# Small squares' additions and a low-part subtraction on VectorE, and a new layout of the period, in a three-layer float32 kernel

## The chip, the cores and the metric

The kernel runs on one core of a Trainium2 chip. A core has a matrix engine (TensorE, PE in the profile; its weight loads are shown apart as PEld), a vector engine (VectorE, DVE), an engine for functions of one operand (ScalarE, ACT), a general one (GpSimd, POOL) and a queue for transfers (SyncE, SP). Each works through its own list of instructions in order, and semaphores tie the lists together. The metric is the device time of one execution in microseconds.

## The reference, cut to what matters

The input x has 8 elements of 512 tokens by 256 channels, all float32. Four residual layers follow one another:

```python
x = x + attn_a(layernorm(x))   # 16 heads of 64, attention among the 64 channels of one token's head
x = x + ffn(layernorm(x))      # silu gate 256->1024, two gelu layers 1024->1024, 1024->256
x = x + attn_b(layernorm(x))   # ordinary causal attention over 512 tokens, 16 heads of 16
x = x + ffn(layernorm(x))
```

The first attention is the unusual one. For every token and head it forms a 64 by 64 matrix of products q[i]*k[j], keeps the lower triangle (j <= i), takes its softmax along j and multiplies by v:

```python
scores = einsum('bshq,bshk->bshqk', Q, K);  scores[upper triangle] = -inf
attn   = einsum('bshqk,bshk->bshq', softmax(scores), V)
```

This is no matrix product: each token has a triangle of its own, so nearly all of it is elementwise work on VectorE, GpSimd and ScalarE. The other layers are mostly matrix products.

## The kernel before

**Tiles and periods.** In the first attention, 128 tokens lie on the 128 partitions. A *period* is the work on one tile of 128 tokens (i, 4 per element) and one group of 4 heads (g, 4 per element). So an element b has 16 periods, and the kernel 128. Element 0 uses one layout (`'first'`), elements 1 to 7 another (`'order'`).

**Squares.** The triangle is cut into its diagonal and squares below it: in each head one square of 32 by 32, two of 16, four of 8, and so on to 32 of 1. `units` (line 597) packs them in four units: unit 0 is the squares of 32 of heads 0 and 1, unit 1 the squares of 16 of all four heads, unit 2 the squares of 32 of heads 2 and 3, and unit 3 all squares of 8, 4, 2 and 1. For each unit the steps are `scores` (products q*k; on GpSimd for units 0, 1 and 2, on VectorE for unit 3), `exps` (ScalarE), `weigh` (times v, on VectorE), then the sums along j. The tile `acc` gathers for each query the denominator (half 0) and the numerator (half 1).

**Sums.** Units 0 to 2 are first halved by `halve`, an adding DMA that GpSimd issues (line 861). After that:
- Unit 0 has the kind `'pe16'` (`'sum': ['pe16', 'dve']`): `sums32` adds by 16 transposing matmuls into PSUM (line 882), ScalarE copies (944), PE transposes back (953), and VectorE's `add32` adds the PSUM result into `acc` (964).
- Unit 2 has the kind `'dve'` in elements 1 to 7: `fold` on GpSimd (869), `gather` on VectorE (1002), addition on GpSimd through `adds` and `add_rows` (1016). In element 0 it is `'pe16'` as well.
- Unit 1: `gather` on VectorE, and `adds` on GpSimd.
- Unit 3: squares of 8 and 4 go through `gather` on VectorE and `adds` on GpSimd. For those of 2 and 1, `small_squares` needs no reduction: GpSimd adds the two halves of the squares of 2 (line 987) and adds both results into `acc` (line 1016, rows named `acc<-acc,ws`).

Then `invert` (a reciprocal on VectorE, 1022), `divide` (GpSimd, 1028), two transposes on PE (`turn_group`, 1038), and the output projection (`project_out`, `new_x`). All transposes and projections of this layer share one PSUM tile, `bank`, of two halves.

**The order.** The program is written out by a table. An entry `[slot, what, ...]` says that this step of period n is issued in slot 12*n + slot. All periods overlap, and within one slot the steps go in the order of the table:

```python
n, r = divmod(t - slot, 12)
if r == 0 and lo <= n < hi:
    now.append((place / len(order), what, self.todo[n] + args))
```

Between the slots a generator hands out the other three layers of the previous element (`after_a`, line 1534), paced so that they keep step with the periods; in one element the PE passes through gate products (1229), hidden products (1301), the second attention (1380 to 1503), then a second gate and hidden stretch. An engine's queue is therefore the interleaving of both, fixed when the program is built.

**The gate.** For each of 8 blocks of a feed-forward layer, ScalarE takes silu (1205), VectorE multiplies (1208), ScalarE rounds a high part (1212), and the low part, what was lost in rounding, is a subtraction of 128x512 (1213), on GpSimd. `later` puts each of these steps one flush after the one before. The same pattern in the hidden layers has its subtraction on VectorE (1267).

Of the kernel before, what the change touches and what calls it, by code (L numbers as in the profile page):

```python
# [13 lines left out]
ALU = mybir.AluOpType  # L14
# [5 lines left out]
NB, S, D = 8, 512, 256  # L20
# [22 lines left out]
G = {'sum': ['pe16', 'dve'],  # L43
 'p16': 2,
 'rot': 4,
 'half': [0, 0, 0, 0, 1, 1],
 'order': [[12, 'weigh', 2], [10, 'exps', 2], [17, 'turn16'], [23, 'add32', 0], [24, 'adds', 3],
           [6, 'halve', 0], [6, 'scores', 2, 0, 2], [27, 'add16'], [-120, 'load'], [23, 'add32', 2],
           [32, 'turn_group'], [20, 'gather', 3], [-30, 'ahead'], [22, 'small_squares'], [16, 'sums16'],
           [8, 'scores', 2, 1, 2], [25, 'invert'], [9, 'weigh', 1], [-22, 'turn_x'], [-25, 'normalise'],  # L50
           [17, 'fold', 2], [20, 'turn_sums', 2], [12, 'halve', 2], [12, 'exps', 3], [-22, 'keep_x'],
           [13, 'weigh', 3], [11, 'scores', 3, 0, 1], [20, 'sums32', 2], [5, 'weigh', 0], [34, 'project_out'],
           [12, 'sums32', 0], [-1, 'scores', 0, 0, 2], [37, 'new_x'], [-6, 'project'], [6, 'exps', 1],
           [15, 'turn_sums', 0], [-5, 'keep_qk'], [4, 'scores', 1, 1, 2], [3, 'exps', 0], [15, 'keep16'],
           [18, 'keep_sums', 2], [32, 'keep_att'], [27, 'divide'], [1, 'scores', 1, 0, 2],
           [0, 'scores', 0, 1, 2], [15, 'gather', 1], [16, 'fold', 0], [16, 'adds', 1], [10, 'halve', 1],
           [14, 'keep_sums', 0]],
 'first': {'sum': ['pe16', 'pe16'],
           'p16': 2,
           'sum16': 'dve',  # L60
           'order': [[15, 'weigh', 3], [26, 'divide'], [7, 'scores', 2, 1, 2], [12, 'weigh', 2],
                     [10, 'halve', 1], [6, 'scores', 2, 0, 2], [20, 'gather', 3], [6, 'halve', 0],
                     [34, 'project_out'], [6, 'exps', 1], [21, 'small_squares'], [18, 'turn_sums', 0],
                     [15, 'keep16'], [11, 'scores', 3, 0, 1], [9, 'weigh', 1], [20, 'sums32', 2],
                     [-120, 'load'], [33, 'keep_att'], [-30, 'ahead'], [12, 'halve', 2], [22, 'adds', 3],
                     [-1, 'scores', 0, 0, 2], [16, 'fold', 2], [25, 'add16'], [16, 'adds', 1], [36, 'new_x'],
                     [14, 'exps', 3], [14, 'sums16'], [22, 'turn_sums', 2], [2, 'scores', 1, 0, 2],
                     [17, 'fold', 0], [23, 'add32', 2], [-22, 'turn_x'], [19, 'turn16'], [-5, 'keep_qk'],
                     [15, 'gather', 1], [21, 'keep_sums', 2], [0, 'scores', 0, 1, 2], [24, 'invert'],
                     [15, 'keep_sums', 0], [9, 'exps', 2], [-21, 'keep_x'], [4, 'weigh', 0],  # L70
                     [31, 'turn_group'], [-25, 'normalise'], [14, 'sums32', 0], [3, 'scores', 1, 1, 2],
                     [-9, 'project'], [3, 'exps', 0], [19, 'add32', 0]]},
 'sum16': 'dve'}


@with_exitstack
# [241 lines left out]
def fast_path(ctx: ExitStack, tc: tile.TileContext, k, t, flag):  # L318

    nc = tc.nc  # L320
# [37 lines left out]
    for g in range(NG):  # L358
# [4 lines left out]
        else:  # L363
            both = block(f"fit_{g}")
# [142 lines left out]
        yield  # L507
        yield from bound_scores()

    def bias_row(ps, j):  # L510

        nc.tensor.matmul(ps, biases[j][:, D:], biases[j][:, :D], start=False, stop=False)

    def plus(ps, xi):

        nc.tensor.matmul(ps, ident, xi, start=False, stop=True)
# [14 lines left out]
    def bank_half(j):  # L531
        return bank[:, j, :]
# [78 lines left out]
    def kind(b, n_u):  # L611
        c = G["first"] if b == 0 and "first" in G else G
        return c["sum"][n_u // 2] if n_u in (0, 2) else c.get("sum16", "dve")

    def p16(b):
        return (G["first"] if b == 0 and "first" in G else G)["p16"]
# [56 lines left out]
    class AttentionA:  # L673
# [118 lines left out]
        def scores(self, b, i, g, n_u, part, parts):  # L792

            qv, kt = self.live[b, i, g][:2]
            if n_u == 0 and part == 0:
                acc = ap_.tile([P, 2, GW], F32, tag="acc", name=f"acc_{b}_{i}_{g}", bufs=3)
                self.live[b, i, g].append(acc)
                nc.vector.tensor_tensor(acc[:, 0, :], qv[:, 0], kt[:, 0], ALU.mult)
                self.done[b, i, g] = 1
            if part == 0:  # L800
                if n_u < NU - 1 and (n_u != 1 or G["rot"] == 4):
                    w = wt.tile([P, 4096], F32, tag="w", name=f"w_{b}_{i}_{g}_{n_u}", bufs=G["rot"])
                elif n_u == 1:
                    w = wt.tile([P, 4096], F32, tag="w16", name=f"w16_{b}_{i}_{g}")
                else:
                    w = wt.tile([P, 2 * SMALL], F32, tag="ws", name=f"ws_{b}_{i}_{g}")
                self.live[b, i, g, n_u] = w
                self.ps = []
                for n, off, nsq, cols in squares(units[n_u]):
                    self.ps += list(pieces(w, n, off, nsq, cols, b, n_u, 2))  # L810
                if not hasattr(self, "pieces"): self.pieces = {}
                self.pieces[b, i, g, n_u] = self.ps
            ps = self.pieces[b, i, g, n_u]
            on_pool = n_u in (0, 2) or (n_u == 1 and part < p16(b))
            eng, q = (nc.gpsimd, kt[:, 1]) if on_pool else (nc.vector, qv[:, 0])
            mine = ps if parts == 1 else [ps[part]]
            for e, ev, rows, columns in mine:
                shape = list(e.shape)
                eng.tensor_tensor(  # L819
                    e, rows(q).to_broadcast(shape), columns(kt[:, 0]).to_broadcast(shape), ALU.mult  # L820
                )
            self.got(b, i, g, n_u, "p", part, parts)
# [155 lines left out]
        def small_squares(self, b, i, g):  # L978

            assert (b, i, g, NU - 1, "w") in self.seen  # L980
            self.seen.add((b, i, g, NU - 1, "s"))
            w = self.live[b, i, g, NU - 1]
            for n, off, nsq, cols in squares(units[NU - 1]):
                if n <= 2:
                    both = self.columns_of(w, n, off, nsq)
                    if n == 2:
                        nc.gpsimd.tensor_tensor(both[..., :1], both[..., :1], both[..., 1:], ALU.add)
                    self.add_rows(b, i, g, n, cols, both[..., 0])
            if (b, i, g, NU - 1, "r") in self.seen: self.live.pop((b, i, g, NU - 1))

        def gather(self, b, i, g, n_u):
# [13 lines left out]
        def adds(self, b, i, g, n_u):  # L1005
            if n_u == 1 and kind(b, 1) != "dve": return
            for args in self.sums.pop((b, i, g, n_u)):
                self.add_rows(*args)

        def add_rows(self, b, i, g, n, cols, part):  # L1010

            self.done[b, i, g] += 1
            assert (b, i, g, 0, 'w') in self.seen
            acc = self.live[b, i, g][2]
            rows = acc[:, :, cols].rearrange("p a (x t) -> p a x t", t=2 * n)[..., n:]
            nc.gpsimd.tensor_tensor(rows, rows, part.rearrange("p a (x i) -> p a x i", i=n), ALU.add)  # L1016

        def invert(self, b, i, g):
            acc = self.live[b, i, g][2]
# [4 lines left out]
        def divide(self, b, i, g):  # L1024
            acc = self.live[b, i, g][2]
            assert (b, i, g, "i") in self.seen
            self.seen.add((b, i, g, "d"))
            (nc.vector if G.get("div") else nc.gpsimd).tensor_tensor(acc[:, 1, :], acc[:, 1, :], acc[:, 0, :], ALU.mult)

        def turn_group(self, b, i, g):  # L1030
            acc = self.live.pop((b, i, g))[2]
# [13 lines left out]
        def project_out(self, b, i, g):  # L1045

            att, nch = self.live.pop("att"), GW // P
            assert "pta" not in self.live
            self.take(G["half"][3], 0, 1)
            po = bank_half(G["half"][3])  # L1050
            for c in range(nch):
                nc.tensor.matmul(
                    po, att[:, c, :], self.wo[b, g][:, c, :], start=(c == 0), stop=False
                )
            if g == 0:
                bias_row(po, 0)
            plus(po, self.x[b][:, i, :])
            if i == NT - 1:
                self.load_wo(b + (g + 1) // NG, (g + 1) % NG)
            self.live["po"] = po  # L1060

        def new_x(self, b, i, g):
            nc.scalar.copy(self.x[b][:, i, :], self.live.pop("po"))
            self.free(G["half"][3], 0, 1)
            if g == NG - 1:
                self.ready.add((b, i))
# [500 lines left out]
    with tc.manual_schedule(engines={ET.PE, ET.DVE, ET.Activation, ET.Pool}):  # L1567
        a = AttentionA()
# [125 lines left out]
```

## Time and profile before

| | |
|---|---|
| time, median of 3 runs (lowest to highest) | 3785.21 us (3784.87 to 3791.1) |
| the profiled execution's own time | 3788.55 us |
| its span, first to last instruction | 3786.5 us |
| mean granted TensorE clock | 0.892 |
| periods of element 4 (1746.2 to 2189.5 us) | 16, 443.3 us |

The times of the table are from runs of the whole kernel; the span and everything below the first row comes from one execution taken by the profiler. A line of the profile reads "line, engine, operation, output<-input, shape, count | busy us, mean ns | idle time of the engine just before, and what ended it". A wait "A <- B" means that engine and line A stood idle until B ended. An engine that is idle for other reasons than its own work can still be what everyone else waits for.

The kernel has a head (until some 60 us), element 0 of the first attention alone (to 430 us), a long middle in which the first attention of one element runs beside the other layers of the one before (to some 3490 us), and a tail with the last element's other layers. The steps touched by the change lie in the middle; the period's layout also in element 0.

### The profile page before, as it was taken

To read this page: it belongs to the slowest core of one execution; us is meant where nothing else is said; L and a number is where in the kernel's file an instruction comes from. 1 tells how busy PE (TensorE), PEld (TensorE's weight loads), DVE (VectorE), ACT (ScalarE), POOL (GpSimd) and SP (SyncE) were. 2 spreads that over 40 slices of the span, in tenths; PEclk is the share of its full clock that TensorE was granted. 3 is DMA by queue.
4 is the path that set the end of the run, shared out by engine and by line. 5 is a ranking of instruction groups with operands and counts; after the bars stand their busy time and mean duration, and the time that the engine had idled before them with its cause. 6 is when DMAs were issued, how large, how long until landed. Compare 5 with 4: busy or idle time off the path is not lost.

```text
span 3786.5 us, 42405 instructions
## 1 busy us (share of the span) xinstructions
PE 3070.3 (81%) x14464; PEld 2205.1 (58%) x14464; DVE 3031.7 (80%) x3506; ACT 2440.7 (64%) x3432; POOL 3177.1 (84%) x3020
## 2 busy tenths in 40 slices
PE   6766597788987888778877888779887789778998
PEld 3454474476745666466644666457664567547757
DVE  6889888888888888888888888888888788787216
ACT  3544476587766776677765767658766677656453
POOL 6888899999899998998999898988989889897211
PEclk7777699898988989889998999989998899879999
DMA  8777787687876878778876787768787688768414
GB/s 232 172 145 154 168 204 168 131 210 195 201 167 151 221 190 194 145 178 204 214 159 140 197 199 188 167 141 222 187 195 147 160 204 202 163 133 221 139 48 173
DMA packets 117327, 665.74 MB, mean 176 GB/s; under 512 B 12775, under 2 KB 30826, under 8 KB 43756
## 3 DMA queue, kind: packets, MB, share of 16 engines
q0 software_dynamic: 80640, 587.24, 67.6%
q1 hardware_dynamic: 36460, 75.69, 5.9%
q8 instruction: 117, 1.92, 0.2%
q14 instruction: 110, 0.89, 0.1%
HBM read 251.58 MB, written 8.65 MB: 69 GB/s over the span
## 4 chain that ended last, share of the span: by engine, by line
POOL 34%; PE 28%; ACT 12%; DVE 11%; issue 9%; DMA 6%; POOLq 0%; ACTq 0%; DVEq 0%; SPq 0%
POOL w L819 17%; PE ph L1301 10%; DMA w<-w 6%; POOL acc L1016 4%; DVE w L854 4%; PE bank L882 4%; POOL w L869 3%; ACT w L842 3%; DVE ws L819 3%; POOL h L1213 2%; PE pw L1229 2%; POOL w L861 2%; PE pyb L1459 2%; PE psb L1447 1%; PE qv L772 1%
## 5 line engine op out<-in xcount | busy, mean ns | idle before, releaser
L819 POOL TENSOR_TENSOR w<-k 128x1024 f32<-128x1024 f32 x768 | 1681.1, 2285 | 18.4 <-PE bank L882 10.6
L1301 PE MATMUL ph<-h,hidden 128*128 128x512 f32 x4096 | 1045.7, 410 | 53.2 <-POOL h L1213 49.5
L1301 PEld LDWEIGHTS ph<-h,hidden 128*128 128x128 f32 x4096 | 781.5, 194 | 239.5 <-POOL h L1213 55.5
L842 ACT ACTIVATE w<-w 128x2048 f32<-128x2048 f32 x384 | 733.9, 1912 | 281.8 <-POOL w L819 279.8
L854 DVE TENSOR_TENSOR w<-w,qv 128x1024 f32<-128x1024 f32 (+1 forms) x624 | 890.5, 1459 | 16.4 <-ACT w L842 16.4
L861 POOL DMA_DIRECT2D w<-w x384 | 361.6, 942 | 209.1 <-DVE w L854 135.0
L882 PE MATMUL bank<-ident,w 128*128 128x128 f32 x2304 | 365.2, 326 | 165.1 <-DVE acc L964 83.3
L1016 POOL TENSOR_TENSOR acc<-acc,red 128x256 f32<-128x256 f32 x496 | 428.2, 863 | 27.7 <-DVE red L1002 16.4
L882 PEld LDWEIGHTS bank<-ident,w 128*128 128x128 f32 x2304 | 332.5, 172 | 203.0 <-DVE acc L964 114.9
L1002 DVE TENSOR_REDUCE red<-w 128x256 f32<-128x2048 f32 x240 | 427.1, 1780 | 10.7 <-DMA w<-w 8.9
L1002 DVE TENSOR_REDUCE red<-ws 128x256 f32<-128x2048 f32 (+1 forms) x256 | 435.4, 1742 | 0.0
L842 ACT ACTIVATE ws<-ws 128x1920 f32<-128x1920 f32 x128 | 231.7, 1810 | 184.8 <-DVE ws L819 179.4
L1229 PE MATMUL pw<-xnt,gate 128*128 128x512 f32 (+2 forms) x1152 | 287.8, 403 | 48.1 <-ACT silu L1205 16.8
L869 POOL TENSOR_TENSOR w<-w 128x1024 f32<-128x1024 f32 x112 | 287.1, 2564 | 20.9 <-DMA w<-w 20.8
L819 DVE TENSOR_TENSOR ws<-qv,k 128x1024 f32<-128x1024 f32 (+3 forms) x512 | 300.2, 649 | 3.9 <-POOL acc L1016 3.9
L1267 DVE TENSOR_TENSOR h<-ph,h 128x512 fp32r<-128x512 f32 x256 | 170.8, 687 | 164.3 <-ACT ph L1263 158.5
L854 DVE TENSOR_TENSOR ws<-ws,qv 128x1024 f32<-128x1024 f32 (+3 forms) x512 | 292.1, 633 | 0.0
L1229 PEld LDWEIGHTS pw<-xnt,gate 128*128 128x128 f32 x1152 | 213.6, 201 | 104.9 <-ACT silu L1205 23.3
L772 PE MATMUL qv<-wqv,xnta 128*128 128x512 f32 x512 | 252.8, 618 | 12.2 <-DVE ws L854 11.3
L964 DVE TENSOR_TENSOR acc<-acc,bank 128x128 f32<-128x128 f32 x144 | 41.4, 287 | 256.2 <-POOL acc L1016 162.7
L1022 DVE RECIPROCAL acc<-acc 128x256 f32<-128x256 f32 x128 | 223.5, 1746 | 24.8 <-POOL acc L1016 24.7
L1262 ACT ACTIVATE h<-ph,s_sb 128x512 fp32r<-128x512 f32 x256 | 176.4, 689 | 99.9 <-PE ph L1301 98.0
(162 smaller groups left out, 5116.4 us busy)
## 6 DMA issues: line engine op xcount, KB each, us to landing
w<-w POOLq DMA_DIRECT2D x384, 1024.0 KB, 7.6
hidden<-in_h POOLq DMA_DIRECT2D x128, 1024.0 KB, 6.4
gate<-in_w12p POOLq DMA_DIRECT2D x32, 1024.0 KB, 5.9
w<-in_w3p POOLq DMA_DIRECT2D x16, 1024.0 KB, 5.5
wqv<-wqv_d SPq DMA_DIRECT2D x31, 512.0 KB, 4.8
wo<-in_wo SPq DMA_DIRECT2D x32, 256.0 KB, 3.9
w<-in_h SPq DMA_DIRECT2D x8, 1024.0 KB, 6.8
wk<-wk_d SPq DMA_DIRECT2D x31, 256.0 KB, 3.0
```

The source lines that it names most:

```text
L772: nc.tensor.matmul(qv.rearrange("p j f -> p (j f)"), xnt[:, c, :], wqv[:, c, :], start=(c == 0), stop=(c == DC - 1),)
L819: eng.tensor_tensor(e, rows(q).to_broadcast(shape), columns(kt[:, 0]).to_broadcast(shape), ALU.mult)
L842: nc.scalar.activation(e, e, AF.Exp, scale=C**-0.5)
L854: nc.vector.tensor_tensor(ev, e, columns(qv[:, 1]).to_broadcast(list(e.shape)), ALU.mult)
L861: nc.gpsimd.dma_start(w[:, :2048], w[:, 2048:], accum_op=ALU.add)
L869: nc.gpsimd.tensor_tensor(w[:, :1024], w[:, :1024], w[:, 1024:2048], ALU.add)
L882: nc.tensor.matmul(bank_half(G["half"][4])[:, :P], w[:, j * P : (j + 1) * P], ident, start=(j == 0), stop=(j == n - 1), is_transpose=True,)
L1002: nc.vector.tensor_reduce(red, self.columns_of(w, n, off, nsq), AX.X, ALU.add)
L1016: nc.gpsimd.tensor_tensor(rows, rows, part.rearrange("p a (x i) -> p a x i", i=n), ALU.add)
L1022: nc.vector.reciprocal(acc[:, 0, :], acc[:, 0, :])
L1229: nc.tensor.matmul(pj[:, toks], w[:, m % 4, j, c, :], xs[:, p, c, toks], start=(p == 0 and c == 0), stop=(p == 1 and c == DC - 1),)
L1301: nc.tensor.matmul(pss[j], w[:, j, c, :], h_in(p, c), start=(p == 0 and c == 0), stop=(p == 1 and c == MC - 1),)
```

## The change

Three things are set in the table `G`, and a few functions learn to read them:
- `'on': ['adds0', 'small']` for elements 1 to 7 and `'on': []` for element 0. A step whose name is in the list uses VectorE instead of GpSimd. `small` covers the halving of the squares of 2 and the two additions in `small_squares`. `adds0` is asked for in `add_rows` when called from `adds` for unit 0.
- `'lo': 'dve'`: the gate's low part (line 1213 before) is on VectorE, in all elements.
- Both tables `'order'` are written anew: slots and places within slots differ.

`project_out` puts the bias row first instead of last in g == 0. The remaining branches (`P3`, `div`, `plusx`) name options that are not set.

```diff
- 'order': [[12, 'weigh', 2], [10, 'exps', 2], [17, 'turn16'], [23, 'add32', 0], [24, 'adds', 3],
-           [6, 'halve', 0], [6, 'scores', 2, 0, 2], [27, 'add16'], [-120, 'load'], [23, 'add32', 2],
-           [32, 'turn_group'], [20, 'gather', 3], [-30, 'ahead'], [22, 'small_squares'], [16, 'sums16'],
-           [8, 'scores', 2, 1, 2], [25, 'invert'], [9, 'weigh', 1], [-22, 'turn_x'], [-25, 'normalise'],
-           [17, 'fold', 2], [20, 'turn_sums', 2], [12, 'halve', 2], [12, 'exps', 3], [-22, 'keep_x'],
-           [13, 'weigh', 3], [11, 'scores', 3, 0, 1], [20, 'sums32', 2], [5, 'weigh', 0], [34, 'project_out'],
-           [12, 'sums32', 0], [-1, 'scores', 0, 0, 2], [37, 'new_x'], [-6, 'project'], [6, 'exps', 1],
-           [15, 'turn_sums', 0], [-5, 'keep_qk'], [4, 'scores', 1, 1, 2], [3, 'exps', 0], [15, 'keep16'],
-           [18, 'keep_sums', 2], [32, 'keep_att'], [27, 'divide'], [1, 'scores', 1, 0, 2],
-           [0, 'scores', 0, 1, 2], [15, 'gather', 1], [16, 'fold', 0], [16, 'adds', 1], [10, 'halve', 1],
-           [14, 'keep_sums', 0]],
+ 'order': [[12, 'weigh', 2], [12, 'exps', 3], [23, 'add32', 0], [15, 'gather', 1], [24, 'adds', 3],
+           [6, 'halve', 0], [6, 'scores', 2, 0, 2], [6, 'scores', 2, 1, 2], [-22, 'turn_x'], [-120, 'load'],
+           [16, 'keep_sums', 2], [23, 'add32', 2], [17, 'sums16'], [25, 'invert'], [-27, 'normalise'],
+           [12, 'halve', 2], [20, 'gather', 3], [-30, 'ahead'], [-22, 'keep_x'], [37, 'new_x'],
+           [32, 'turn_group'], [21, 'turn16'], [-5, 'project'], [15, 'turn_sums', 0], [10, 'exps', 2],
+           [34, 'project_out'], [17, 'fold', 2], [12, 'sums32', 0], [9, 'weigh', 1], [20, 'sums32', 2],
+           [13, 'weigh', 3], [-2, 'scores', 0, 0, 2], [3, 'scores', 1, 1, 2], [3, 'exps', 0],
+           [1, 'scores', 1, 0, 2], [35, 'add16'], [18, 'turn_sums', 2], [13, 'fold', 0], [14, 'keep_sums', 0],
+           [16, 'keep16'], [7, 'exps', 1], [25, 'divide'], [4, 'weigh', 0], [11, 'scores', 3, 0, 1],
+           [-5, 'keep_qk'], [32, 'keep_att'], [0, 'scores', 0, 1, 2], [10, 'halve', 1], [22, 'small_squares'],
+           [16, 'adds', 1]],
...
- 'first': 'order': [... [18, 'turn_sums', 0], ... [31, 'turn_group'], ... [3, 'scores', 1, 1, 2], ... [19, 'add32', 0]]
+ 'first': 'order': [... [16, 'turn_sums', 0], ... [32, 'turn_group'], ... [2, 'scores', 1, 1, 2], ... [19, 'add32', 0]], 'on': []
...
- 'sum16': 'dve'}
+ 'sum16': 'dve',
+ 'on': ['adds0', 'small'],
+ 'lo': 'dve'}
...
+    def on(b):
+        return (G["first"] if b == 0 and "first" in G else G).get("on", [])
...
         def small_squares(self, b, i, g):
...
                     if n == 2:
-                        nc.gpsimd.tensor_tensor(both[..., :1], both[..., :1], both[..., 1:], ALU.add)
-                    self.add_rows(b, i, g, n, cols, both[..., 0])
+                        (nc.vector if "small" in on(b) else nc.gpsimd).tensor_tensor(both[..., :1], both[..., :1], both[..., 1:], ALU.add)
+                    self.add_rows(b, i, g, n, cols, both[..., 0], "small")
...
         def adds(self, b, i, g, n_u):
...
-                self.add_rows(*args)
+                self.add_rows(*args, f"adds{n_u}")
...
-            nc.gpsimd.tensor_tensor(rows, rows, part.rearrange("p a (x i) -> p a x i", i=n), ALU.add)
+            (nc.vector if what in on(b) else nc.gpsimd).tensor_tensor(rows, rows, part.rearrange("p a (x i) -> p a x i", i=n), ALU.add)
...
         def project_out(self, b, i, g):
...
+            if g == 0:
+                bias_row(po, 0, True)
             for c in range(nch):
                 nc.tensor.matmul(
-                    po, att[:, c, :], self.wo[b, g][:, c, :], start=(c == 0), stop=False
+                    po, att[:, c, :], self.wo[b, g][:, c, :], start=(c == 0 and g > 0), stop=(c == nch - 1 and G.get("plusx") == "dve")
                 )
-            if g == 0:
-                bias_row(po, 0)
-            plus(po, self.x[b][:, i, :])
+            if G.get("plusx") != "dve":
+                plus(po, self.x[b][:, i, :])
```

More of the change, by code (lines that the diff above doesn't have):

```diff
@@ L60 @@
            'sum16': 'dve',
[L61 to L72, printed above, removed]
@@ L73 @@
- 'sum16': 'dve'}
+           'order': [[26, 'divide'], [25, 'invert'], [15, 'weigh', 3], [22, 'turn_sums', 2], [36, 'new_x'],
+                     [12, 'weigh', 2], [10, 'halve', 1], [18, 'fold', 0], [6, 'scores', 2, 0, 2],
+                     [-1, 'scores', 0, 0, 2], [6, 'halve', 0], [-5, 'keep_qk'], [13, 'sums16'],
+                     [-1, 'scores', 0, 1, 2], [15, 'gather', 1], [6, 'scores', 2, 1, 2], [15, 'keep_sums', 0],
+                     [6, 'exps', 1], [-120, 'load'], [-28, 'normalise'], [-30, 'ahead'], [16, 'turn_sums', 0],
+                     [20, 'gather', 3], [13, 'halve', 2], [34, 'project_out'], [11, 'scores', 3, 0, 1],
+                     [17, 'fold', 2], [-22, 'turn_x'], [14, 'exps', 3], [2, 'scores', 1, 0, 2],
+                     [21, 'keep_sums', 2], [29, 'add16'], [-21, 'keep_x'], [5, 'weigh', 0], [33, 'keep_att'],
+                     [21, 'small_squares'], [17, 'adds', 1], [17, 'turn16'], [16, 'keep16'], [23, 'add32', 2],
+                     [14, 'sums32', 0], [22, 'adds', 3], [20, 'sums32', 2], [9, 'weigh', 1],
+                     [32, 'turn_group'], [9, 'exps', 2], [2, 'scores', 1, 1, 2], [-9, 'project'],
+                     [3, 'exps', 0], [19, 'add32', 0]],
@@ L76, in general_path @@
+           'on': []},
+ 'sum16': 'dve',
+ 'on': ['adds0', 'small'],
+ 'lo': 'dve'}
 @with_exitstack
@@ L508, in later_weights, with bias_row @@
         yield from bound_scores()
-    def bias_row(ps, j):
-        nc.tensor.matmul(ps, biases[j][:, D:], biases[j][:, :D], start=False, stop=False)
+    def bias_row(ps, j, start=False):
+        nc.tensor.matmul(ps, biases[j][:, D:], biases[j][:, :D], start=start, stop=False)
     def plus(ps, xi):
@@ L813, in scores @@
             ps = self.pieces[b, i, g, n_u]
-            on_pool = n_u in (0, 2) or (n_u == 1 and part < p16(b))
+            on_pool = n_u in (0, 2) or (n_u == 1 and part < p16(b)) or (n_u == 3 and "P3" in on(b))
             eng, q = (nc.gpsimd, kt[:, 1]) if on_pool else (nc.vector, qv[:, 0])
@@ L1007, in adds, with add_rows @@
             for args in self.sums.pop((b, i, g, n_u)):
-                self.add_rows(*args)
-        def add_rows(self, b, i, g, n, cols, part):
+                self.add_rows(*args, f"adds{n_u}")
+        def add_rows(self, b, i, g, n, cols, part, what):
             self.done[b, i, g] += 1
@@ L1027, in divide @@
             self.seen.add((b, i, g, "d"))
-            (nc.vector if G.get("div") else nc.gpsimd).tensor_tensor(acc[:, 1, :], acc[:, 1, :], acc[:, 0, :], ALU.mult)
+            (nc.vector if "div" in on(b) else nc.gpsimd).tensor_tensor(acc[:, 1, :], acc[:, 1, :], acc[:, 0, :], ALU.mult)
         def turn_group(self, b, i, g):
@@ L1062, in new_x @@
         def new_x(self, b, i, g):
-            nc.scalar.copy(self.x[b][:, i, :], self.live.pop("po"))
+            if G.get("plusx") == "dve":
+                nc.vector.tensor_tensor(self.x[b][:, i, :], self.x[b][:, i, :], self.live.pop("po"), ALU.add)
+            else:
+                nc.scalar.copy(self.x[b][:, i, :], self.live.pop("po"))
             self.free(G["half"][3], 0, 1)
```

## The prediction

> **What bounds the kernel now.** I read the page's busy times first: no engine is full.
>
> ```profile
> PE 3070.3 (81%) x14464; PEld 2205.1 (58%) x14464; DVE 3031.7 (80%) x3506; ACT 2440.7 (64%) x3432; POOL 3177.1 (84%) x3020
> ```
>
> So the average hides stages. I cut the middle into periods at the starts of the reciprocals (line 1022) and asked for the engines' busy times in some of them; columns are PE, PEld, DVE, ACT, POOL, then TensorE's clock and DMA.
>
> ```profile
> 1993.20:2016.40 23.20, 18.38 (x134) 9.18 (x126) 20.50 (x23) 16.90 (x32) 21.89 (x18) 0.85 0.69 139
> 1777.70:1810.40 32.70, 28.52 (x120) 21.27 (x118) 25.94 (x31) 25.96 (x34) 31.89 (x28) 0.95 0.70 163
> 1865.20:1890.10 24.90, 22.22 (x100) 17.52 (x99) 23.04 (x27) 19.64 (x23) 22.56 (x20) 1.00 0.96 248
> 1890.10:1921.50 31.40, 25.09 (x118) 18.37 (x117) 24.00 (x33) 20.09 (x30) 26.93 (x34) 0.95 0.63 138
> 295.90:318.10 22.20, 12.65 (x58) 9.47 (x57) 19.61 (x22) 9.36 (x11) 19.32 (x16) 0.81 0.70 142
> ```
>
> Beside the second attention (row 1) GpSimd is the bound, 21.9 of 23.2 us; beside a gate (row 2) too, 31.9 of 32.7. Beside hidden products (row 3) GpSimd, VectorE and PE are nearly level. At the seam (row 4) and in element 0 (row 5) no engine is full: waits bound these.
>
> Next, who VectorE waits for, in the window 500 to 3400 us (2900 us, 105.5 periods of 27.5 us; VectorE busy 2446, GpSimd 2632, PE 2392 by the sums of windows):
>
> ```profile
> DVE acc L964 <- POOL acc L1016: 144.1, 59, 7.0
> DVE h L1267 <- ACT ph L1263: 89.8, 93, 6.0
> DVE silu L1208 <- ACT silu L1205: 64.5, 26, 5.7
> DVE acc L964 <- PE bank L516: 54.8, 34, 4.2
> DVE xnt L1160 <- ACT xnt L1153: 43.2, 26, 2.9
> DVE acc L1022 <- POOL acc L1016: 20.9, 13, 2.6
> ```
>
> The largest is `add32` waiting until GpSimd has added the small squares into the same `acc`. In the chain of waits this is a handover back and forth:
>
> ```profile
> 1939.21 0.66 POOL ws L987
> 1939.86 0.07 issue
> 1939.93 0.84 POOL acc L1016
> 1940.85 0.75 POOL acc L1016
> 1941.62 0.29 DVE acc L964
> ```
>
> PE in turn stood 68.3 us in this window until `add32` freed `bank`.
>
> [...] 2285 ns against 1219 for 1024 products (line 819), 795 against 415 at 256 elements. [...] Line 987 took 0.60 us in one period and 1.14 in another, but no row here ties this to VectorE.
>
> **The change, part by part.**
>
> ```profile
> L1016 POOL TENSOR_TENSOR acc<-acc,ws 128x256 f32<-128x256 f32 x210 | 167.0, 795 | 16.5
> L1213 POOL TENSOR_TENSOR h<-silu,h 128x512 fp32r<-128x512 f32 x96 | 144.6, 1601 | 6.9 <-ACT h L1212 6.9
> L987 POOL TENSOR_TENSOR ws<-ws 128x256 f32<-128x256 f32 x105 | 101.7, 968 | 0.1
> L819 DVE TENSOR_TENSOR ws<-qv,k 128x512 f32<-128x512 f32 x105 | 71.5, 681 | 0.0
> L819 DVE TENSOR_TENSOR ws<-qv,k 128x256 f32<-128x256 f32 x105 | 43.6, 415 | 0.0
> ```
>
> 1. *`adds0` moves nothing.* Unit 0 has the kind `'pe16'`, so its sum never goes through `adds`; `add32` was on VectorE already. The built program agrees: VectorE's list grows by 464 instructions, which is 112 periods x 3 small ones plus 128 gate subtractions.
> 2. *Small squares.* GpSimd loses 101.7 + 167.0 = 269 us in the window, 2.55 per period. VectorE gains 105 x 3 x 0.415 = 131 us, 1.25 per period. In VectorE's list they stand right ahead of `add32`, where it stalled for GpSimd 1.37 us per period (144.1/105.5): the stall is the cover.
> 3. *Gate subtraction.* GpSimd loses 144.6 us; VectorE gains 96 x 0.681 = 65 us. In a period like row 2, which holds 7 of them (11.0 us by its windows), VectorE goes to 25.9 + 1.25 + 7 x 0.69 = 32.0: it takes GpSimd's place as the bound, at nearly the same time. It adds a wait on ScalarE's rounding, with all of VectorE's queue (products, weighing, the reciprocal) behind it. The like wait of line 1208 was 64.5/96 = 0.67 us each; below nothing it cannot go, since VectorE never waited here. Bounds 0 to 0.67; I take 0.26, for ScalarE gets earlier (below).
> 4. *Waits that go.* `add32` and the reciprocal on GpSimd, 165 us: for `add32` nothing of GpSimd's is left just ahead, and the reciprocal waits for three additions with weighing and unit 3's products (4.8 us) in between. The wait of `add32` on PE's line 516, 34 times 1.6 us, shrinks by the 1.25 us now ahead of it: 42 off.
> 5. *Layout, elements 1 to 7.* `project` goes from slot -6 to -5. In PE's list `turn_group` then follows it directly, where some twelve hidden products stood between; it waits until ScalarE has copied k out of `bank`, behind an exponential of 1.9 us (line 842). PE lost 57.6 us this way; I take 0.5 us more per period, bounds 0 and 1.9. Only beside hidden products, where PE has little slack, does it reach the end. Unit 2's second products go from slot 8 to 6, which lets its exponential follow sooner; ScalarE waited 205.1 us on GpSimd's products. No transfer's size changes; the weight loads issued in `project` go along on SP's queue one slot later, and the halving DMAs on GpSimd's queue, 7.6 us to landing, have at least as much time in slots as before. I put these at nothing.
> 6. *Layout, element 0.* `turn_group` goes from slot 31 to 32, past `add32` of slot 19. VectorE waited on it 2.2 us a period (12 times, 27.6 us). GpSimd has 2.6 us of stalls of its own in this period, all on VectorE or ScalarE. I take 0.7 x 12 = 8 us off, bounds 0 and 27. The bias row's place moves no time.
>
> **The sum, twice.** *By waits:* VectorE's 2446 + 131 + 65 = 2642 leaves 258 us of idle time at which the window would stay at 2900. Today's 454, less 165 and 42, is 247: all but no gain if every other wait stays. But the three ScalarE waits (89.8 + 64.5 + 43.2 = 197) come from ScalarE running behind GpSimd, which gets 413 us lighter, and an engine that becomes the last one finds its inputs ready. I halve them: 2642 + 49 + 99 + 25 for the new wait = 2815, so 85 off, or 90 over 112 periods. *By stages,* per element: the five periods beside the second attention (118.6 us) come down from GpSimd's 22 to VectorE's 20.5 + 1.25 = 21.7 plus waits, 5 off; four gate periods (130.9), 4 off; six hidden ones (162.4), nothing, VectorE 24.9 and PE's extra stall against what PE no longer waits for `add32`; the seam (31.4), 1 off. That is 10 x 7 = 70. With element 0: 78 to 98 off. I take 88: from the profiled execution's own 3788.55 this gives 3700 us. That execution lies 3.3 us above the median of the runs, so against the median it would be 3697; the difference is nothing beside the range.
>
> **Rivals.**
> - *Forecast, 3700 (own range 3655 to 3760), chance 0.46.*
> - *Tight packing, 3630, chance 0.22.* As the last engine VectorE keeps almost no waits: 2642 plus 90 is 168 off in the window, 178 over all, less the PE stalls, here 30, and element 0's 8. For: one hidden period (1669.6 to 1693.6 us) already has VectorE busy 22.97 of 24.0 us. Against: seam and gate bound by chains.
> - *Slower, VectorE's queue, 3825, chance 0.24.* The ScalarE waits stay whole and the gate subtraction waits like line 1208 (0.57 us, 55 in all): 2642 + 247 + 55 = 2944, 44 more, 47 over 112 periods, less 8 for element 0. It decides once VectorE idles over 258 us in this window. For: VectorE has 93% in the hidden periods and its list is in order. Against: ScalarE's two longest waits, on GpSimd's and VectorE's products, are of the kind that shrinks.
> - *No change, 3785, chance 0.08.* GpSimd's relief is real, but VectorE's own path fills the time exactly; for this speaks the 247 against 258.
>
> **How the numbers follow.** A change within 0.2% (8 us) cannot be told from none. Faster: forecast and tight packing, and 0.02 of no change, 0.70. Slower: 0.24. Same: 0.06. The range goes from 3625, the tight case, to 3810, short of the slower case's own point, leaving some 0.2 outside; the unknown of step 3 (up to 0.41 x 96 = 39 us more) and of step 5 lie in it.
>
> **What would show it.** VectorE's busy time should be near 3259 us and GpSimd's near 2700 (3177.1 less 112 x 2.55 for the small ones and 192.6 for all gate subtractions). The wait of `add32` on GpSimd should be gone and that on line 516 small; periods beside the second attention near 22 us; element 0's near 21.5. Wrong would be: VectorE's waits on ScalarE grown, gate periods no shorter than 32 us, or PE standing longer at `turn_group`. If VectorE idles more than 258 us in the like window, the slower case holds.

## The result, and the profile after

The changed kernel took 3804.11 us (median of 5 runs, 3795.69 to 3812.64) against 3785.21 us before (3784.87 to 3791.1): a ratio of 1.005, 95% interval 1.003 to 1.0071. It is slower by half a per cent, where 3700 us and faster were forecast. The profiled execution has a span of 3810.4 us. Its busy times:

```profile
PE 3034.0 (80%) x14464; PEld 2181.8 (57%) x14464; DVE 3392.3 (89%) x3970; ACT 2440.4 (64%) x3432; POOL 2787.3 (73%) x2556
```

VectorE was to have 3259 us and has 133 more; GpSimd was to have 2700 us and has 2787, so it has shed 390 us of the 478 that were meant. Lines of the code behind the change have moved: `add32` is 970 now (964 before), the halving of the small squares 993 (987), `add_rows` 1022 (1016), the reciprocal 1028 (1022), the gate's product 1218 (1208), rounding 1222 (1212) and subtraction 1223 (1213).

Whom VectorE waits for, in the same window of 500 to 3400 us (total us, times, longest):

```profile
DVE h L1277 <- ACT ph L1273: 38.2, 56, 4.5
DVE xnt L1170 <- ACT xnt L1163: 26.7, 14, 2.5
...
DVE acc L970 <- PE bank L519: 13.5, 10, 2.6
...
DVE acc L1028 <- POOL acc L1022: 9.2, 7, 1.6
DVE silu L1218 <- ACT silu L1215: 7.0, 5, 2.1
...
DVE h L1223 <- ACT h L1222: 4.0, 7, 0.9
```

The wait of `add32` on GpSimd, 144.1 us before, is gone; the other large ones have shrunk, and the new wait of the gate subtraction on ScalarE is all but nothing. So the loss is not in waits that the profile shows. Three stretches like those shown of before: a period beside the second attention, the long gate period, one of element 0 (columns PE, PEld, DVE, ACT, POOL, then clock and DMA).

```profile
2004.00:2027.70 23.70, 19.24 (x137) 9.54 (x135) 23.31 (x26) 17.08 (x32) 19.76 (x15) 0.86 0.71 144
1781.00:1821.10 40.10, 30.05 (x114) 21.74 (x113) 39.70 (x42) 26.09 (x34) 21.38 (x17) 0.83 0.60 142
276.90:297.50 20.60, 10.38 (x52) 7.70 (x51) 19.62 (x22) 9.35 (x11) 19.21 (x17) 0.91 0.76 153
```

VectorE is full in the first two: 23.3 of 23.7 us where 21.7 of some 22 were expected, and 39.7 of 40.1 where 32.0 were. Element 0 gained more than expected (20.6 us where 21.5 was forecast). Where VectorE's time comes from shows in the groups of instructions (busy us and mean ns of one after the bar, then idle time before them):

```profile
L1223 DVE TENSOR_TENSOR h<-silu,h 128x512 fp32r<-128x512 f32 x96 | 141.2, 1471 | 4.0 <-ACT h L1222 4.0
L993 DVE TENSOR_TENSOR ws<-ws 128x256 f32<-128x256 f32 x104 | 117.0, 1125 | 0.0
L1022 DVE TENSOR_TENSOR acc<-acc,ws 128x256 f32<-128x256 f32 x207 | 88.3, 427 | 7.1
```

The additions of line 1022 took the 0.42 us that were put in. The halvings took 1.13 us instead of 0.415, the gate subtractions 1.47 instead of 0.681. Their own lists say that this is a mean of two kinds (shortest, median, longest in ns):

```profile
L993 DVE TENSOR_TENSOR ws<-ws x112: 407/422/3294, 402.6 to 3516.2; 128x256 f32<-128x256 f32 x112
```

```profile
L1223 DVE TENSOR_TENSOR h<-silu,h x128: 672/681/7058, 448.9 to 3735.8; 128x512 fp32r<-128x512 f32 x128
```

Undisturbed they take what was forecast. Some take far longer, up to 3.29 and 7.06 us. One of these in the timeline (start, us, engine and instruction, in brackets the idle time before it), in the long gate period:

```profile
1789.99 2.65 POOL L875 TENSOR_TENSOR w<-w 128x1024 f32<-128x1024 f32 x1
...
1790.90 7.03 DVE L1223 TENSOR_TENSOR h<-silu,h 128x512 fp32r<-128x512 f32 x1
...
1792.95 4.42 POOL L825 TENSOR_TENSOR w<-k 128x1024 f32<-128x1024 f32 x2
...
1797.85 0.74 DVE L1218 SCALAR_TENSOR_TENSOR silu<-pw,s_sb,silu 128x512 f32<-128x512 f32 x1
...
1798.62 0.62 ACT L1222 CAST h<-silu 128x512 fp32r<-128x512 f32 x1 [8.03 <-DVE silu L1218]
...
1798.64 1.65 PE L1239 MATMUL pw<-xnt,gate 128*128 128x512 f32 x3 [6.80 <-DVE silu L1218]
```

The subtraction starts 0.9 us into a GpSimd addition and ends 0.56 us after the last of GpSimd's two products behind it (1792.95 + 4.42 = 1797.37); between addition and products GpSimd issues a DMA. ScalarE and PE stand 8.0 and 6.8 us for the gate product that is queued behind it on VectorE. The same in a period beside the second attention:

```profile
2015.25 6.33 POOL L825 TENSOR_TENSOR w<-k 128x1024 f32<-128x1024 f32 x3
...
2019.93 1.95 DVE L993 TENSOR_TENSOR ws<-ws 128x256 f32<-128x256 f32 x1
...
2021.92 0.89 DVE L1022 TENSOR_TENSOR acc<-acc,ws 128x256 f32<-128x256 f32 x2
```

The halving ends 0.30 us after GpSimd's run (2021.58). Counted over the whole trace (held: over 15% above the undisturbed time), 50 of 112 halvings and 22 of 128 subtractions were held; in the median these ended 0.29 and 0.56 us after the end of a GpSimd operation. Together the two groups took 76 + 85 = 161 us over their undisturbed durations. All 22 held subtractions and 47 of the 50 held halvings began while GpSimd computed. The other three halvings began while it issued a DMA, 0.05 to 0.31 us ahead of one of its products, and took 2.56 to 2.80 us, each ending 0.29 us behind the end of that product. Both groups read two operands from SBUF, as GpSimd does; VectorE's products and weighing, which read one operand from PSUM, show nothing of the kind (the 128 products of 1024 elements, line 825, lie between 1.21 and 1.22 us, the 480 weighings of 1024 elements, line 860, between 1.19 and 1.22). The two additions of line 1022 also read two operands from SBUF, but they stand right behind the halving, which has already waited: of 224, 37 began while GpSimd computed, 35 of these with 0.05 us or less of its instruction left, and none was held.

Element 3 as a whole, in the same columns as above; before, then after:

```profile
1306.10:1746.20 440.10, 365.83 (x1753) 263.90 (x1752) 372.35 (x435) 310.69 (x431) 401.65 (x379) 0.91 0.78 182
```

```profile
1302.90:1751.30 448.40, 363.96 (x1754) 260.18 (x1753) 422.01 (x500) 310.02 (x431) 349.43 (x315) 0.92 0.76 179
```

VectorE gained 49.7 us of work in an element, where the moved instructions at their undisturbed times are 16 x (3 x 0.415 + 0.681) = 30.8. It went from 85% to 94% of the element and became the bound.

### The profile page after: what moved, and what is told of

Same layout as the page of the kernel before. It is cut to its first block, busy times and chain, and to the rows that moved or that the text cites. A ratio compares the mean times of both kernels' runs of the same rounds, so it can differ in the third digit from the quotient of the medians.

```text
span 3810.4 us, 42369 instructions
## 1 busy us (share of the span) xinstructions
PE 3034.0 (80%) x14464; PEld 2181.8 (57%) x14464; DVE 3392.3 (89%) x3970; ACT 2440.4 (64%) x3432; POOL 2787.3 (73%) x2556
## 4 chain that ended last, share of the span: by engine, by line
DVE 33%; PE 26%; POOL 14%; ACT 13%; issue 10%; DMA 4%; DVEq 0%; ACTq 0%; POOLq 0%; SPq 0%
DVE w L860 8%; PE ph L1311 8%; DVE red L1008 8%; POOL w L825 7%; PE bank L888 4%; DMA w<-w 4%; ACT w L848 3%; DVE ws L825 3%; PE pw L1239 2%; DVE ws L993 2%; DVE h L1223 2%; DVE ws L860 2%; PE pyb L1469 2%; PE qv L778 2%; DVE acc L1022 2%
## 5 line engine op out<-in xcount | busy, mean ns | idle before, releaser
L825 POOL TENSOR_TENSOR w<-k 128x1024 f32<-128x1024 f32 x768 | 1639.8, 2276 | 133.5 <-DVE red L1008 86.8
L1311 PE MATMUL ph<-h,hidden 128*128 128x512 f32 x4096 | 1013.1, 402 | 5.3 <-DMA hidden<-in_h 4.3
L1311 PEld LDWEIGHTS ph<-h,hidden 128*128 128x128 f32 x4096 | 766.7, 190 | 177.4 <-issue 13.1
L867 POOL DMA_DIRECT2D w<-w x384 | 388.6, 1012 | 416.0 <-DVE w L860 242.7
L1022 POOL TENSOR_TENSOR acc<-acc,red 128x256 f32<-128x256 f32 x496 | 374.6, 755 | 128.3 <-DVE acc L1022 74.9
L1239 PE MATMUL pw<-xnt,gate 128*128 128x512 f32 (+2 forms) x1152 | 297.6, 408 | 103.9 <-DVE silu L1218 77.3
L1464 ACT ACTIVATE eb<-psb 128x512 f32<-128x512 f32 (+3 forms) x503 | 180.3, 449 | 96.1 <-PE psb L1461 95.7
```

What stands on the lines that cost most here:

```text
L825: eng.tensor_tensor(e, rows(q).to_broadcast(shape), columns(kt[:, 0]).to_broadcast(shape), ALU.mult)
L867: nc.gpsimd.dma_start(w[:, :2048], w[:, 2048:], accum_op=ALU.add)
L1022: (nc.vector if what in on(b) else nc.gpsimd).tensor_tensor(rows, rows, part.rearrange("p a (x i) -> p a x i", i=n), ALU.add)
L1239: nc.tensor.matmul(pj[:, toks], w[:, m % 4, j, c, :], xs[:, p, c, toks], start=(p == 0 and c == 0), stop=(p == 1 and c == DC - 1),)
L1311: nc.tensor.matmul(pss[j], w[:, j, c, :], h_in(p, c), start=(p == 0 and c == 0), stop=(p == 1 and c == MC - 1),)
```

## The experiments

The theories that the expectations name are three. H: VectorE's additions of two SBUF operands are held while GpSimd computes, and this costs the time. L: the new order of the period costs it. W: nothing but the amount of work on VectorE counts. All ratios are against the kernel before on the same chip.

**The layout alone (e1_layout), with the small squares alone (e2_small), with the gate alone (e3_low).** All have both new orders. The edit of e1 to the kernel after:

```diff
- 'on': ['adds0', 'small'],
- 'lo': 'dve'}
+ 'on': []}
```

e2 has `'on': ['small']}` in that place, e3 `'on': [], 'lo': 'dve'}`.

> The new layout alone: small squares and gate subtraction stay on GpSimd. Theory H (held): an instruction of VectorE with two SBUF inputs stands still until GpSimd's running work ends, and that excess (some 160 us in the changed kernel's trace), not the layout, made it slower. H expects element 0's gain of 20 us to stay and the middle near the kernel before: 3745 to 3785 us, no VectorE instruction of any line lengthened. Theory L (layout): the new order itself costs in the middle; it expects 3795 us or more. Theory W (work): VectorE simply has too much work, whatever its inputs; it expects the same as H here.

> New layout, small squares on VectorE, gate subtraction on GpSimd. H: the halving of the squares of 2 stays lengthened (mean near 1.1 us against 0.42), the gate subtraction's 83 us of excess go; periods beside the second attention stay near 23.7 us, the long gate periods come down from 40 to 31 to 34 us; 3735 to 3775 us. W: VectorE loses only 128 x 0.68 = 87 us of work, so at most that much goes, and no instruction's length changes. L: 3795 us or more.

> New layout, gate subtraction on VectorE, small squares on GpSimd. H: the gate subtraction stays lengthened (mean over 1.2 us against 0.68), the long gate periods stay near 38 to 40 us, the periods beside the second attention return to GpSimd's 23.1; 3770 to 3805 us. W: VectorE loses 112 x 1.25 = 140 us of work against the changed kernel, 3690 to 3730 us. L: 3795 us or more.

| | us, median (lowest to highest) | ratio, interval |
|---|---|---|
| e1_layout | 3963.98 (3958.45 to 3969.28) | 1.0463, 1.0449 to 1.0478 |
| e2_small | 3785.44 (3776.27 to 3792.87) | 0.9989, 0.998 to 0.9997 |
| e3_low | 4001.27 (3999.19 to 4005.23) | 1.0562, 1.0548 to 1.0577 |

What H expected of the times of e1 and e3 was missed by far, and so was W's; L had both at 3795 us or more. VectorE's waits in e1, window 500 to 3400 us:

```profile
DVE acc L969 <- POOL acc L1021: 400.1, 96, 8.8
```

Where GpSimd keeps the small squares, `add32` (969 here) waits 400 us for them instead of 144. The new order issues the first half of unit 0's product at slot -2, ahead in the table of the small squares of an earlier period (slot 22 is slot -2 of the second period after it), so GpSimd does it first. That this entry is what costs here is argued: it was not moved by itself with the small squares on GpSimd. The order is fitted to a VectorE that does the small squares: L holds in that sense, and the times of e1 and e3 say nothing of H. The trace of e3 does: 38 of its 128 gate subtractions were held (1477 ns mean in the window of 500 to 3400 us), as H expected. In e2, with the small squares moved, the halvings are held too (1238 ns mean); it is about as fast as before, 10 us above H's range, and the gate subtraction costs 0.6% on top of it (to after's 1.005), which W allows as well.

**The subtraction with one operand in PSUM (e4_low_psum).** The kernel after, but the gate's product stays in its PSUM tile; ScalarE rounds it from there, and VectorE subtracts from there, later in the list (`lows` is emptied at the next block).

```diff
-                nc.vector.scalar_tensor_tensor(x, p2, s_sb[:, 1, m : m + 1], x, ALU.mult, ALU.mult)
-                later(high)
-
-            def high():
-                nc.scalar.copy(h(0, m), x)
-                later(lambda: (nc.vector if G.get("lo") == "dve" else nc.gpsimd).tensor_tensor(h(1, m), x, h(0, m), ALU.subtract))
+                nc.vector.scalar_tensor_tensor(p2, p2, s_sb[:, 1, m : m + 1], x, ALU.mult, ALU.mult)
+                nc.scalar.copy(h(0, m), p2)
+                lows.append(lambda: nc.vector.tensor_tensor(h(1, m), p2, h(0, m), ALU.subtract))
...
```

> The changed kernel, with the gate's product left in PSUM, so that the subtraction on VectorE reads one operand from PSUM and one from SBUF; as many VectorE instructions and elements as in the changed kernel, and ScalarE's rounding one flush earlier. H: the subtraction takes 0.68 to 0.75 us every time, its 83 us of excess go, the long gate periods come down from 40 to 32 to 35 us; 3715 to 3750 us. W and L: VectorE's work and the layout are those of the changed kernel, so 3795 to 3810 us.

3799.04 us (3789.07 to 3803.79), ratio 1.0018, 1.0005 to 1.003. The group in the window:

```profile
L1226 DVE TENSOR_TENSOR h<-pw,h 128x512 fp32r<-128x512 f32 x96 | 65.0, 685 | 28.5 <-ACT h L1225 28.3
```

No subtraction was held any more, though 55 began while GpSimd computed: for this group the mechanism of H is right. The size is not. Of the 85 us of held time only some 12 reached the end (0.32%, 1.005 to 1.0018), and the total lies where W and L had it. The halvings were still held (49 of 112, 1060 ns mean), and the subtraction now waits for ScalarE.

**The moves in the old order (f1_ops_only), element 0's order alone (f2_first_only).** f1 is before with `'on': ['small'], 'lo': 'dve'` and no new order; f2 is before with the new table of element 0.

> The two moves (the small squares' additions and the gate's subtraction on VectorE in elements 1 to 7) in the order of the kernel before, element 0's order too. H (a VectorE addition or subtraction of two SBUF operands is held until GpSimd's run of instructions ends): the held time stays, near 1.1 us for each halving of the small squares and 1.4 us for each gate subtraction, so 3790 to 3860 us, with element 0 at 371 us as before. L (the new layout is what costs): without it the moves are worth what the sum of waits said, 3690 to 3760 us. W (only the amount of work counts): the same work as after, without element 0's 20 us, so 3815 to 3830 us, at undisturbed durations.

> The kernel before with the new order of element 0 alone; elements 1 to 7 as before. All theories: element 0 falls from 372 to 351 to 353 us and nothing else changes, 3762 to 3775 us. If element 0's gain is taken back at its seam to element 1, 3780 to 3790 us.

f1: 3833.2 us (3828.7 to 3836.62), 1.0115, 1.01 to 1.0129. In the old order the halvings are hardly held (486 ns mean), the gate subtractions as in the kernel after (1647 ns). H had put the time here and W close by (3815 to 3830), so the time doesn't tell them apart; of the durations W had neither group lengthened, and H had the halvings wrong (1.1 us). L, which had the time below 3760, falls: against f1 the new orders are worth 0.65%, 25 us, 17 of them element 0's, so it isn't they as a whole that made the change lose. f2: 3769.14 us (3762.23 to 3776.77), 0.9954, 0.9941 to 0.9967. Element 0's order by itself is worth 0.46%, 17 us.

**Unit 0's first half a slot later (f3_scores_later), and that with e4's edit (f4_scores_later_psum).** In the order of the kernel after, one number:

```diff
-           [13, 'weigh', 3], [-2, 'scores', 0, 0, 2], [3, 'scores', 1, 1, 2], [3, 'exps', 0],
+           [13, 'weigh', 3], [-1, 'scores', 0, 0, 2], [3, 'scores', 1, 1, 2], [3, 'exps', 0],
```

> The kernel after with the first half of unit 0's product one slot later (-2 to -1), so that GpSimd reaches it after the small squares and is not within a long run of products when they begin. H: the halvings of the small squares fall from a mean of 1125 to 450 to 700 ns, the periods beside the second attention from 23.7 to 22.3 to 23.2 us, the total to 3745 to 3785 us. W: the same work, so the total stays at 3800 to 3810 us. L: an order fitted to the moves is disturbed, 3810 us or more.

> Both cures at once: unit 0's first half a slot later, and the gate's product left in PSUM so that the subtraction has one PSUM operand. H: neither group is lengthened (near 0.69 us for the subtractions, 0.45 to 0.7 us for the halvings), 3735 to 3780 us. W and L: 3795 us or more.

f3: 3784.54 us (3776.68 to 3799.34), 0.9994, 0.9983 to 1.0006. f4: 3762.51 us (3760.97 to 3775.55), 0.9939, 0.9924 to 0.9954. The halvings in f3, by their own list:

```profile
L993 DVE TENSOR_TENSOR ws<-ws x112: 393/418/1576, 395.1 to 3481.8; 128x256 f32<-128x256 f32 x112
```

The longest is 1.58 us instead of 3.29, the time above the undisturbed one 10 us instead of 76, at the same work in the same list of VectorE: W falls, and H has a price, 21 us from this one slot, at the upper end of what H expected. (The slot also changes the order of GpSimd's own products; what that alone does was not tried.) f4's groups:

```profile
L1226 DVE TENSOR_TENSOR h<-pw,h 128x512 fp32r<-128x512 f32 x101 | 68.5, 685 | 31.2 <-ACT h L1225 31.1
...
L993 DVE TENSOR_TENSOR ws<-ws 128x256 f32<-128x256 f32 x105 | 51.0, 486 | 0.0
```

With one hold gone and the other all but gone (21 halvings held, 8 us in all), 42 us of after's time are gone, and the kernel is faster than before, within what H expected. The edit that gave some 12 us in e4 gives 21 here; with the intervals of the four runs the two are not told apart. An element of f4 in the columns of the windows:

```profile
1282.00:1725.00 443.00, 368.98 (x1752) 266.52 (x1752) 402.24 (x500) 310.33 (x431) 348.67 (x315) 0.90 0.78 181
```

VectorE has 402.2 us here, 29.9 more than before: near the 30.8 of the moved instructions. But the long gate period stays long:

```profile
1757.50:1794.70 37.20, 29.10 (x107) 21.21 (x107) 32.05 (x42) 25.60 (x34) 21.00 (x17) 0.86 0.59 141
```

VectorE's 32.05 us is what the prediction said (32.0). The period takes 37.2 us, against 32.7 before. Waits in it, of VectorE and of ScalarE:

```profile
DVE h L1226 <- ACT h L1225: 3.1, 3, 1.8
DVE w L860 <- ACT w L848: 1.0, 1, 1.0
DVE pw L1224 <- ACT silu L1221: 0.9, 1, 0.9
```

```profile
ACT h L1225 <- DVE pw L1224: 7.5, 5, 3.2
ACT ws L848 <- DVE ws L825: 3.5, 1, 3.5
```

By these waits VectorE and ScalarE now hand each block of the gate to one another, product, rounding, subtraction, and each stands for the other.

**The small squares alone, with little of the hold, in the new order (g1_later_small) and in the old (g2_old_small).** g1 is f3 without `'lo': 'dve'`; g2 is f2 with `'on': ['small']` in elements 1 to 7.

> The kernel after with unit 0's first half a slot later and the gate's subtraction on GpSimd again, so of the two moves the small squares' alone. H: no instruction is held for long, 3740 to 3770 us; the gate periods (four in an element) come back from 144.6 to 131 to 133 us, the five beside the second attention stay at 117 us. Rival (GpSimd needs to be rid of the subtraction): gate periods stay at 138 us or more, total 3785 us or more.

> The order of the kernel before in elements 1 to 7, element 0's new order, and of the two moves the small squares' alone. H: the small squares are held little in this order (10 us in all, as with both moves), so it is faster than with element 0's new order alone (3769 us) by 5 to 25 us: 3740 to 3765 us. L (the old order does not suit the move): 3770 us or more.

g1: 3740.74 us (3736.1 to 3748.75), 0.9861, 0.9845 to 0.9877. g2: 3747.42 us (3744.32 to 3750.83), 0.988, 0.9864 to 0.9896. Both beat both kernels. Of the halvings, 27 were held in g1 and 24 in g2, 15 and 14 us in all. Against f2 the small squares' move is worth 0.74%, 28 us, in the old order (g2); g1, with the new order as well, is not told apart from g2. Of the two moves it is the gate subtraction that loses: f3 is g1 with it, and 1.3% slower; f4 is g1 with it and no hold of it, and 0.8% slower.

**The hold by itself (e6_probe_sbuf, e7_probe_psum).** The kernel before with one more VectorE product, whose result nobody reads, behind unit 1's weighing in elements 1 to 7. The two differ in where one operand lies: `kt` is in SBUF, `qv` in PSUM. In e6:

```diff
+            if n_u == 1 and b > 0:
+                nc.vector.tensor_tensor(probe, kt[:, 1, :192], kt[:, 0, :192], ALU.mult)
...
```

e7 has `qv[:, 0, :192]` as the first operand.

> The kernel before plus one VectorE product of 192 elements in a period of elements 1 to 7, both inputs in SBUF, nothing waiting for its result; undisturbed 0.35 us. H: where GpSimd computes when it starts it ends about 0.3 us after GpSimd's run; mean above 0.6 us, some of 1 to 4 us. W: all near 0.35 us.

> The same product at the same place, one of its inputs in PSUM and the other in SBUF. H and W: all 0.35 to 0.40 us, also where GpSimd computes when it starts.

One run each, 3788.58 and 3794.8 us, beside 3791.21 of before. The probes by their lists, e6 and then e7 (shortest, median, longest ns):

```profile
L857 DVE TENSOR_TENSOR probe<-k x112: 349/599/2821, 395.4 to 3469.1; 128x192 f32<-128x192 f32 x112
```

```profile
L857 DVE TENSOR_TENSOR probe<-qv,k x112: 346/351/357, 402.5 to 3471.9; 128x192 f32<-128x192 f32 x112
```

The same place in the timelines of the two, again e6 first:

```profile
3436.97 4.01 POOL L1216 TENSOR_TENSOR h<-silu,h 128x512 fp32r<-128x512 f32 x3
3438.95 2.82 DVE L857 TENSOR_TENSOR probe<-k 128x192 f32<-128x192 f32 x1
3440.73 0.82 POOL L990 TENSOR_TENSOR ws<-ws 128x256 f32<-128x256 f32 x1
```

```profile
3439.92 4.01 POOL L1216 TENSOR_TENSOR h<-silu,h 128x512 fp32r<-128x512 f32 x3
3441.89 0.35 DVE L857 TENSOR_TENSOR probe<-qv,k 128x192 f32<-128x192 f32 x1
```

About 2 us into the same run of three GpSimd subtractions, the probe with both operands in SBUF takes 2.82 us, the other 0.35. In e7, 105 of the 112 began while GpSimd computed and none was lengthened; in e6, where as many did, 78 were (716 ns mean of all). That is what H expected of both, but for one point: a held probe need not wait for the end of GpSimd's run. 38 of the 78 ended between two GpSimd instructions, the second of which began 0.08 us after the first.

## Why the prediction was wrong, point by point

A chain of runs, each one step from the last, splits the result:

| | ratio | step, of 3785 us |
|---|---|---|
| before | 1 | |
| element 0's order (f2) | 0.9954 | -17 |
| elements 1 to 7: small squares on VectorE (g2) | 0.9880 | -28 |
| elements 1 to 7: new order, but unit 0's half at slot -1 (g1) | 0.9861 | -7, not clear of noise |
| gate subtraction on VectorE (f3) | 0.9994 | +50 |
| unit 0's half at slot -2 (after) | 1.0050 | +21 |

1. *`adds0` moves nothing*: right, VectorE has the 464 instructions more.
2. *Small squares*: the stall of `add32` right. The prediction's pairs, 2285 against 1219 ns at 1024 elements and 795 against 415 at 256, are GpSimd's and VectorE's times in the profile of before. GpSimd's side was put too large, for both moves together: its records overlap in time, so those of the moved instructions add up to 489 us in the trace of before, while without them its busy time there is only 382 us less (390 were measured). The price on VectorE, 3 x 0.415 us, is the first failed term: the halving took 1.125 us in the mean, because it was held. It costs 21 us by the last row.
3. *Gate subtraction*: 0.681 us each is the second failed term; it took 1.47. Without the hold (f4 against f3, 0.55%) 21 us come back. The remaining 30 us (f4 against g1, 0.78%) are no matter of the hold. That VectorE takes GpSimd's place "at nearly the same time" held for the busy time, 32.0 us, but not for the period, 37.2 us; the waits suggest that it is because VectorE's list now alternates with ScalarE's where GpSimd's subtraction had been beside both. How much of the 30 us this makes stays open: between the profiled executions of g1 and f4 an element's four gate periods grow by 7 us (131.5 to 138.7), but its six hidden ones shrink by as much (163.5 to 156.1), and 6 to 8 us belong to e4's edit in the tail behind the last period (290.7 us in g1, 292.6 in f3, 298.8 in f4). The new wait on ScalarE was put at 0.26 us each; it was 4.0 us in all in the kernel after, and 0.31 each in f4.
4. *Waits that go*: the three that were named went (`add32` on GpSimd wholly, the reciprocal's from 20.9 to 9.2 us, that on PE's line 516 from 54.8 to 13.5). VectorE was busy for 2730.5 us of the window and idle for 2900 - 2730.5 = 169.5, where 173 were forecast, but that is luck: held time, booked as busy, had filled the idle time. In f4, with both moves and little of the hold, 255 us were idle. The point from which the slower case was to decide, 258, was not reached in the kernel after, and it was slower all the same. The rival had the right sign with the wrong mechanism.
5. *Layout of elements 1 to 7, put at nothing*: wrong. The entry that decides between f3 and the kernel after is not among those weighed there: unit 0's first half from slot -1 to -2. With the small squares left on GpSimd the new orders cost 4.6% (e1), and with them on VectorE this slot is what puts GpSimd in a run of products just when the halving starts. `project` and `turn_group`, on which the step dwelt, were not tried by themselves.
6. *Element 0*: -8 us forecast, -17 measured (f2), inside the bounds of 0 to 27.

By stages, sums per element, means of elements 2 to 6 in the profiled executions: beside the second attention 118.7 to 122.9 us (5 off forecast), four gate periods 131.1 to 140.3 (4 off), six hidden ones 160.3 to 156.1 (no change), the seam 32.2 to 30.7 (1 off). The gate is the largest miss.

Both failed terms have one cause, and the profile of before had a sign of it. All moved instructions have two SBUF inputs, and the prediction charged nothing for what GpSimd does beside them, as no row of before tied the one odd duration (line 987) to VectorE. That duration was indeed another matter: line 987 took 0.61 to 0.63 us where its record began after the GpSimd record before it had ended, and 1.07 to 1.21 where it began 0.5 us or more ahead of that end. But another row showed the price. Apart from a few in the head, VectorE had eleven large instructions with two SBUF inputs before, those of line 1188 in the tail, and one of them began 0.07 us into a run of GpSimd's subtractions:

```profile
3695.68 4.59 POOL L1213 TENSOR_TENSOR h<-silu,h 128x512 fp32r<-128x512 f32 x2 [8.04 <-ACT h L1212]
3695.75 3.37 DVE L1188 TENSOR_TENSOR w<-w,gate 128x2048 f32<-128x2048 f32 x1
```

It took 3.37 us, the other ten 2.28 to 2.31. A cost seen once was to be bounded from both sides, and the upper bound, a GpSimd run of products, was in the profile. e6 and e7 have the two cases side by side: 2.82 us for the probe with two SBUF inputs, 0.35 for the one with an input in PSUM.

Without the gate's move and with little of the hold, g1 gained 1.4%, 53 us with element 0, and not the 88 that were forecast. So the sum fails in one more term, the waits that were to be halved. A period of g1 beside the second attention, and g1's window of 500 to 3400 us:

```profile
1937.46:1961.00 23.54, 19.18 (x145) 9.20 (x141) 21.93 (x25) 16.25 (x31) 19.75 (x15) 0.90 0.79 172
500.00:3400.00 2900.00, 2399.02 (x11539) 1715.40 (x11537) 2603.41 (x3163) 2025.81 (x2834) 2419.81 (x2174) 0.91 0.77 180
```

VectorE's work in the period is close to the 21.7 us of the sum by stages, yet the period takes 23.5 us and not some 22. In the window VectorE is idle for 297 us, where 49 + 99 = 148 were left without the gate's new wait: the three waits on ScalarE fell from 197 to 146 us only. So elements 2 to 6 are no shorter, 444.1 us each in g1's profiled execution (the slowest of its four) and 442.4 before; what g1 gained there lies in element 0 (27 us), element 1 (8) and element 7 (10). What bounds the elements between was not tried, and stays open.

## What to carry to other kernels

An instruction's price went with its operands' places here: beside the same GpSimd run the probe took 2.82 us with both operands in SBUF and 0.35 with one in PSUM (e6, e7). Before moving work from GpSimd to VectorE, count its SBUF inputs: a subtraction of 0.68 us with two of them took up to 7.03 us, held behind what GpSimd was computing (the kernel after), and then the work removed from GpSimd is not the only thing to look at but also what GpSimd does in its place at that moment. If it must move, give it one operand from PSUM (in e4 none of the subtractions was held any more), or issue it where GpSimd is in no run of products (in f3 the halvings' held time fell from 76 to 10 us); and a table tuned for one placement is not to be judged with another.

## What the runs showed of the hardware

- A hold can outlast the GpSimd instruction in progress. In the kernel after a 0.68 us subtraction took 7.03 us, across the rest of one GpSimd addition and two products behind it. It need not outlast it: 38 of the 78 held probes of e6 ended between two GpSimd instructions 0.08 us apart. What decides this was not tried.
- GpSimd was held too. Two probes of e6 that began within 0.01 us of a GpSimd addition took 0.35 us, and the additions 1.07 and 1.08 us, where the median is 0.80. In before, the second of the two subtractions that met line 1188 took 3.21 us, most others near it 1.28; and one that began 0.09 us behind the start of another instruction of line 1188 took 3.35 us, while that one took 2.28.
- Not every GpSimd instruction held one. Nine halvings and probes (three in the kernel after, six in e6) began with 0.37 to 0.40 us left of a GpSimd power of one element per partition (`rstd<-rstd,power`), and took their undisturbed 0.42 and 0.35 us.
- Held instructions ended, in the median, 0.29 us after a GpSimd end for 256 elements in a row (halvings, the kernel after), 0.56 us for 512 (gate subtractions, the kernel after), 0.22 us for 192 (probes, e6).
- The profile books the hold as busy time, not as a wait. It shows in the halvings' mean against their median, 1125 against 422 ns in the kernel after, and nowhere among the waits.
